# VectorE, in place of TensorE, subtracts the row maximum of the odd heads' scores, and the order of all queues is drawn up anew

## The chip, the core and the metric

The kernel runs on one core of a Trainium2 chip, as one launch. The core has five engines, each with an instruction queue of its own that it works off in order: TensorE (PE: matrix products, into the banks of PSUM), VectorE (DVE), ScalarE (ACT), GpSimd (POOL) and SyncE (SP, which here only issues transfers). The metric is the device time of one execution in microseconds (us); lower is better.

## What is computed

The input is 32 sequences of 128 tokens with 128 features. First comes one cross attention (16 heads of 8 features, 4 key heads) on a normed input, and then a stack of six layers. Each layer is a local attention with 16 heads of 64 features and a feed-forward layer. The change touches the softmax of the local attention:

```python
def local_attention(q, k, v):            # windows of 32 tokens
    ...
    bk2, bv2 = (look(bk), look(bv))      # each window sees itself and the one before
    ...
    mask = (it < jb) | (it > jb + w) | (jb == -1)
    sim = jnp.einsum('bhwie,bhwje->bhwij', bq, bk2) * QK_SCALE
    sim = jnp.where(mask, -jnp.finfo(sim.dtype).max, sim)
    attn = jax.nn.softmax(sim, -1)
    out = jnp.einsum('bhwij,bhwje->bhwie', attn, bv2)
```

The kernel takes heads in pairs; what follows calls the second of each pair an odd head. In 64 columns there are the scores of one head's window against its own 32 keys and the 32 before.

## The kernel before

**Tiling.** The stack works on groups of four sequences (eight groups per layer), and within a group on one sequence at a time, a unit: six layers of 32 units, 192 in all. `unit` projects queries and keys (`qk`, lines 442 to 444, three matmuls of 512 columns each that share one bank), squares them on ScalarE (`sq`, L790), multiplies them by the rotary tables on VectorE (`tab`, L796, 1024 columns, the last reader of a projection's bank), adds the halves on GpSimd (`add`, L802), sums the squares on VectorE (`ss`, L805), scales (`mul`, L819), and transposes on TensorE (`tq`, L448). The values come through `y`, `yt` (L837) and a transfer into the tile `ysh`. `ffn` closes a group: residual sum (L907, L967), norm, and three gated products.

**Scores and softmax.** Two banks are set aside for scores, `sc`, one for even heads (`a` = 0) and one for odd heads (`a` = 1). ScalarE first copies the mask into both (`msk`, L860), and the matmuls of `scores` (L855) add to it. `soft(a)` then does the softmax of one bank, 128 rows by eight times 64 columns:

- `mx` (L869, VectorE): the maximum of every 64 columns, with its sign turned, into `mx`.
- Even heads: `exb` (L877, ScalarE): eight exponentials of 64 columns, each with its column of `mx` as bias and with the sum beside it.
- Odd heads (`FOLD = (1,)`): `fold` (L871, TensorE): one matmul of the identity `identr` with `mx`, broadcast to 512 columns, which adds the negative maximum to the scores in their bank. `ex` (L873, ScalarE): one exponential of 512 columns from the bank to the tile `pr`. `sm` (L882, VectorE): the sums.
- Both: reciprocal (`rl`, L883, VectorE), product (`pl`, L884, GpSimd), transpose of 32x32 blocks (`pt`, L886, VectorE). Then `av` (L899, TensorE, 56 small matmuls) multiplies by the values.

The tiles `pr` and `PT` are three each, `mx` four. Projections, transposes and products share five banks, `pj`.

**Order.** No engine's order is the order of the program's text. Each operation is put down as `S.op` with the tiles that it reads and writes; `Sched.run` then plays the whole kernel with a table of costs (`COST`: engine, time for which it holds the engine, time to the result) and writes every engine's queue in the order that this gives. Whenever an engine is free it takes, among the operations that are ready and get their tiles, the one due first. An operation is due at the number of its unit plus a shift from `LATER`, by its name and number (`mx1`) or by its name (`mx`), and 0 if neither is there. `KEEP` says how many of the five shared banks an operation must leave free. Tiles of a pool are given out in the order in which the text asks for them. On the chip the queues are fixed, and semaphores do the waiting.

Of the kernel before, what the change touches and what calls it, by code (L numbers as in the profile page):

```python
# [16 lines left out]
P = 128  # L17
# [10 lines left out]

COST = dict(
    ax=("PE", 0.4, 0.64), axh=("ACT", 0.52, 0.62), axl=("DVE", 0.6, 0.7),  # L30
    qk=("PE", 0.72, 0.94), sq=("ACT", 0.53, 0.63), ss=("DVE", 0.6, 0.68), tab=("DVE", 1.14, 1.22), add=("POOL", 1.27, 1.3), ta=("DVE", .63, .72), adda=("POOL", 1.1, 6),
    mxs=("POOL", 0.25, 0.29), dmx=("DVE", 0.42, 0.5), dnw=("DVE", 0.36, 0.44), ln=("ACT", .2, .24), ep=("ACT", .2, .24), nw=("POOL", 0.31, 0.33),
    mul=("POOL", 1.01, 1.06), tq=("PE", 0.43, 0.66), evq=("ACT", 0.51, 0.61), evk=("ACT", .5, .62),
    y=("PE", 0.72, 0.94), yt=("ACT", 0.52, 0.62), dm=("SP", 0.58, 7.0), xph=("ACT", .6, .7), xpl=("ACT", .6, .7), dw=("SP", .62, 3.5), dr=("SP", .62, 4.5),
    msk=("ACT", 0.54, 0.63), sc0=("PE", .52, .75), sc1=("PE", .52, .75), mx=("DVE", 0.6, 0.68), fold=("PE", 0.3, 0.5), ex=("ACT", .51, .62), exb=("ACT", 1.17, 1.3),
    sm=("DVE", 0.6, 0.68), rl=("DVE", 0.13, 0.21), pl=("POOL", 1.02, 1.06), pt=("DVE", 0.62, 0.7), av=("PE", 1.92, 2.02), sc=("PE", 0.72, 0.9),
    res=("DVE", .63, .72), psh=("SP", 1.65, 3.5), st=("DVE", 0.79, 0.87), ag=("DVE", .35, .40), xn1=("POOL", 1.08, 1.1),
    eps=("POOL", .22, .26), lnf=("ACT", .22, .21), epf=("ACT", .22, .21), nwf=("POOL", 0.18, 0.24), xn=("ACT", 1.55, 1.65), nmr=("POOL", .18, .24), nmg=("POOL", .2, .26), ysq=("ACT", .2, .24), xn2=("POOL", 1.08, 1.1),
    ptn=("PE", .46, .70), xnh=("ACT", .51, .62), xnl=("DVE", .60, .66), gate=("PE", 0.72, 0.93), gel=("ACT", 0.63, 0.7),
    pa=("PE", 0.72, 0.93), um=("DVE", 0.68, 0.76), w2=("PE", 0.67, 0.9), res2=("DVE", .63, .72), xo=("POOL", 1.3, 1.3),  # L40
    io=("SP", .62, 3.5), iox=("SP", 1.1, 4.0), ldw=("SP", 0.5, 4.0),
    bip=("PE", 1.3, 1.5), bid=("DVE", .25, .3), tb=("DVE", 1.1, 1.1), w1a=("ACT", .78, .9), w1b=("ACT", .39, .5),
    w1c=("POOL", .95, .95), qkh=("ACT", .54, .64), qkl=("POOL", 1.3, 1.3), wvp=("PE", .46, .70), wve=("ACT", .49, .60),
    mp=("PE", 0.5, 0.7), mh=("ACT", .28, .38), ml=("DVE", .33, .42),
    xst=("DVE", 0.8, 0.87), xag=("DVE", .30, .35), xnw=("POOL", .20, .20), xtr=("PE", 0.54, 0.68), xev=("ACT", .49, .60),
    xpj=("PE", 0.98, 1.15), hil=("ACT", .58, .70), lof=("DVE", .66, .75), pv=("PE", .90, 1.1), vt=("DVE", .25, .30),
    td=("PE", .90, 1.1), abs=("ACT", .52, .65), lnb=("ACT", .55, .64), mkb=("DVE", .42, .42), tbm=("DVE", .95, 1.0),
    xsc=("PE", 0.4, 0.58), xmx=("DVE", .86, .95), xsb=("POOL", 1.04, 1.07), xex=("ACT", .55, .65), xpa=("PE", 1.1, 1.3),
    xrl=("DVE", 0.17, 0.25), xat=("DVE", .21, .29), pwm=("PE", .90, 1.1), xrs=("DVE", .63, .70),
)  # L50

LATER = dict(y=0.5, iox=1.9, xsc=-0.5, evk=-0.25, tab0=-3.2, pv=1.95, sq2=1.0, xex=1.25, ss1=3.95, rl0=5.15,
    bip=-2.05, add3=3.75, ss2=-1, xpa=0.25, tq2=-2, sq3=0.5, ax=-0.3, tab2=0.75, ysq=1.15, tq1=0.75, gate2=0.6,
    mx1=2.7, mul2=2.5, fold0=-2.5, y3=3.75, exb0=6.3, pl1=4.3, add0=1.25, tq0=2.2, nwf=1.6, msk0=0.7, y1=3.75,
    evq0=-0.7, add1=-0.35, mxs=-1.75, yt2=2.0, td=-0.95, ep=0.5, y0=3.2, gate1=-0.75, xsb=-1.05, mul1=1.3, rl1=3.75,
    qk0=-0.25, ln=-2.5, sq=-0.15, av=2.7, pwm=2.0, evq2=0.3, xpj=-1.25, xmx=3.95, ex1=1.15, y2=2.15, xnl=3, lof=0,
    tq=1.25, mp=-2.9, tab1=3.85, qk2=-1.45, yt3=-0.2, exb01=3.65, exb00=-0.35, qk1=0.4, xrl=-0.75, yt1=1.75, pl0=-1.4,
    sm0=-1.1, ml=-1, xn2=1.0, gel1=0.65, um2=-0.95, gate0=0.1, io=0.5, tab=-0.25, abs=-0.9, add=6.25, pa2=1.75,
    evq1=-0.5, xst=-0.75, xo=4, gel0=3, xag=0.9, gel2=-1.5, xev=3.65, tq3=2.85, pt=3.15, axh=-2, mx0=-0.45, lnb=3.95,
    pa1=0.1, bid=1.45, sq0=0.2, ex=2.05, nw=3.1, yt0=-0.8, ss=3.2, axl=-1.2, xn=0.1, xtr=-1.15, w1a=1.9, dm2=0.75,  # L60
    ss0=-2.15, msk1=-0.95, ldw=1, gate=-1.4, msk=-1.75, lnf=1.75, um1=4.4, vt=-0.25, w1c=-1.3, ss3=-1.5, dm3=3.95,
    tb=1.5, psh=-0.2, fold1=-2.2, tab3=0.15, xn1=0.0, pa=0.35, ptn=-0.65, mx=3.1, exb=0.75, dm1=4, evq3=-1.4,
    evq=3.05, res2=-1.5, xnh=-0.25, wvp=0.4, fold=0.45, rl=-0.95, dm=0.35, epf=-1.9, qk=0.25, pl=-2.1, sm=1.1,
    w2=1.15, sc0=0.0, mul=-0.5, tbm=0.25, mkb=2.6, xrs=-0.75, dnw=-0.5, mh=0.75, um=2, qkl=1.2, um0=-0.25, ag=-0.4,
    mul3=0.2, qkh=-1.55, xat=3, eps=-1.5, nmr=0.0, pa0=3.1, yt=2, gel=0.5, st=0.75, hil=0.05, sq1=-0.75, wve=3,
    nmg=0.75)

KEEP = dict(qk=0, y=0, gate=0, pa=0, xtr=0, xpj=1, pv=1, td=1, xsc=0, wvp=2, mp=2, bip=2, sc0=0, tq=0, ptn=0, ax=0,
    w2=1)
ONEBANK = ("pj", "sc", "po")  # L70
LAT = dict(PE=.06, ACT=.05, DVE=.08, POOL=.16, SP=.08)

# [13 lines left out]
class Sched:  # L86
# [150 lines left out]
def body(ctx: ExitStack, tc: tile.TileContext, x, ctx_in, fside, mask_in, xWq, xWk, xWv, xWo, xtw,  # L237
         Wqkv, q_scale, k_scale, Wo, ln_g, ln_b, W1, b1, W2, b2, cst, x1d, out):
    nc = tc.nc
# [11 lines left out]
    def tl(tag, shape, dt=F32):  # L251
        return mem.tile(shape, dt, tag=tag, name=tag)

    S = Sched()
    S.back = lambda: nc.scalar.preload_act_table_set("natural_log_exp_and_others")  # L255

    def pool(name, n, shape, dt=F32, inorder=True):
        S.pool(name, [lambda d, i=i: tl(f"{name}_{i}_", shape, d or dt) for i in range(n)], inorder)
# [29 lines left out]
        pool(name, 4, [P, 32])  # L288
    for name in ("xm", "sm"):
        pool(name, 6, [P, 8])  # L290
    pool("mx", 4, [P, 8], F32R)
    for name in ("nv", "ny", "nw", "av", "ay", "aw"):
        pool(name, 2, [P, 8])
    for name in ("n", "a"):
# [7 lines left out]
    ident = cs[:, 0:128]  # L302
# [474 lines left out]
    def unit(l, g, j, w, G, pri):  # L777
        xh, xl = G["x"]
        ss = Buf("ss")
        rts = []  # L780
        tab = w["tab"]
# [62 lines left out]
        sc = [Buf("sc"), Buf("sc")]  # L844
# [19 lines left out]
        def r8(b):  # L864
            return b.t.rearrange("p (a c) -> p a c", c=64)

        def soft(a):
            s, mx, pr, sm, PT = sc[a], Buf("mx"), Buf("pr"), Buf("sm"), PTs[a]
            S.op("mx", lambda: nc.vector.tensor_reduce(mx.t, r8(s), axis=AX.X, op=ALU.max, negate=True), pri, [s], [mx], k=a)  # L869
            if a in FOLD:  # L870
                S.op("fold", lambda: nc.tensor.matmul(s.t, identr, mx.t.unsqueeze(2).to_broadcast([P, 8, 64]), start=False,  # L871
                                                      stop=True, skip_group_check=True), pri, [mx, s], [s], k=a)
                S.op("ex", lambda: nc.scalar.activation(pr.t, s.t, AF.Exp), pri, [s], [pr], table="E", k=a)  # L873
            else:
                def pieces(h):
                    for i in range(4 * h, 4 * h + 4):
                        nc.scalar.activation(r8(pr)[:, i], r8(s)[:, i], AF.Exp, bias=mx.t[:, i:i + 1].bitcast(F32),  # L877
                                             accum_out=sm.t[:, i:i + 1])
# [171 lines left out]
```

## Time and profile before

Three runs: median 2971.93 us (2967.31 to 2973.36).

| | |
|---|---|
| profiled execution, its own time | 2971.38 us |
| its span, first to last instruction | 2969.6 us |
| granted TensorE clock, mean | 0.993 |
| `fold` L871, all 192: TensorE busy | 75.97 us |
| `ex` L873, all 192: ScalarE busy | 120.01 us |
| `mx` L869, all 384: VectorE busy | 252.54 us |
| `exb` L877, all 3072: ScalarE busy | 503.28 us |

The profile is of one execution, taken by the hardware. "Busy" is the time covered by an engine's instructions, overlaps counted once; PE stands for the matmuls and PEld for TensorE's weight loads, which overlap them. Matmuls are pipelined and their ends are modelled. In a group of instructions the columns are the line, engine, operation, output and inputs, shapes and number, then the busy time and the mean duration in ns, and then the idle time of the engine just before them with what ended it. The chain that ended last is followed back from the last instruction, at each step to what released it. The cross attention takes about the first 290 us; the six layers follow.

### The profile page before, as it was taken

Reading aid. Unit: us, or ns where it says so; the run is one execution under the profiler, and the core shown is the slowest. Engines: PE = TensorE matmul, PEld = TensorE weight load, DVE = VectorE, ACT = ScalarE, POOL = GpSimd, SP = SyncE. Lnnn points to the kernel's source line nnn. Section 1 sums busy time; section 2 is a strip of 40 time slices with the busy share of each in tenths; the row PEclk is TensorE's granted clock in tenths of the full one; section 3 lists DMA queues with packets and bytes.
Section 4 is the critical chain, followed back from the end, with each engine's and each line's share of the span. In section 5 each row is a group of like instructions: output and inputs, shape, how many; then the busy total and the mean of one; then the engine's idle time right before and its main releaser. Section 6 shows DMA issues by size and latency. Waiting matters only on the chain.

```text
span 2969.6 us, 116618 instructions
## 1 busy us (share of the span) xinstructions
PE 2885.9 (97%) x47695; PEld 2282.8 (77%) x47695; DVE 2522.5 (85%) x5155; ACT 2641.4 (89%) x7679; POOL 2540.0 (86%) x2950
## 2 busy tenths in 40 slices
PE   8999999999999999999999999999999999999997
PEld 5666788787777777787787777777777887877775
DVE  6778988888988888988889888888888888888883
ACT  6887899999989989999999899899899999999885
POOL 7667989888988888989898898888889888899883
PEclk9999999999999999999999999999999999999998
DMA  4101455555645455555455555455555455455453
GB/s 116 33 17 34 85 93 88 81 87 98 99 81 87 80 88 101 95 86 89 78 92 104 84 92 86 74 93 100 87 86 91 76 91 96 80 101 91 81 97 62
DMA packets 216889, 250.84 MB, mean 84 GB/s; under 512 B 90623, under 2 KB 111395, under 8 KB 216355
## 3 DMA queue, kind: packets, MB, share of 16 engines
q1 hardware_dynamic: 215442, 242.94, 48.2%
q8 instruction: 376, 6.16, 1.1%
q14 instruction: 159, 1.29, 0.2%
q10 hardware_dynamic: 912, 0.44, 0.1%
HBM read 25.31 MB, written 4.19 MB: 10 GB/s over the span
## 4 chain that ended last, share of the span: by engine, by line
PE 83%; ACT 6%; DMA 5%; issue 3%; POOL 2%; DVE 2%; SPq 0%; POOLq 0%; DVEq 0%; ACTq 0%
PE bank__68 L899 11%; PE bank__67 L855 4%; PE bank__66 L855 4%; PE bank__61 L448 3%; PE bank__65 L448 3%; PE bank__62 L448 3%; PE bank__63 L448 3%; PE bank__64 L448 3%; PE bank__64 L442 3%; PE bank__65 L442 3%; PE bank__61 L442 3%; PE bank__63 L442 3%; PE bank__62 L442 3%; PE bank__65 L444 2%; PE bank__65 L443 2%
## 5 line engine op out<-in xcount | busy, mean ns | idle before, releaser
L860 ACT COPY bank__66<-mask 128x512 f32<-128x512 f32 x192 | 122.1, 636 | 5.4 <-PE bank__66 L374 4.7
L860 ACT COPY bank__67<-mask 128x512 f32<-128x512 f32 x192 | 122.1, 636 | 1.5 <-PE bank__67 L374 0.9
L255 ACT ACT_TABLE_LOAD x48 | 61.6, 1283 | 0.8
L944 ACT ACT_TABLE_LOAD x48 | 61.6, 1283 | 0.8
L727 ACT ACTIVATE ysh__96<-ysh__96 128x512 f32<-128x512 f32 x64 | 40.9, 639 | 11.7 <-POOL ysh__96 L725 11.4
L907 DVE TENSOR_TENSOR xt<-bank__68,xt 128x512 f32<-128x512 f32 x48 | 32.6, 680 | 11.7 <-PE bank__68 L899 11.7
L727 ACT ACTIVATE wch__97<-wch__97 128x512 f32<-128x512 f32 x16 | 10.1, 633 | 8.8 <-POOL wch__97 L725 8.8
L967 DVE TENSOR_TENSOR xt<-bank__64,xt 128x512 f32<-128x512 f32 x12 | 8.3, 691 | 6.8 <-PE bank__64 L963 6.8
L974 POOL TENSOR_TENSOR raw__50456<-raw__50456,xt 128x512 f32<-128x512 f32 x1 | 1.3, 1261 | 13.9 <-DVE xt L967 13.9
L727 ACT ACTIVATE wch__98<-wch__98 128x512 f32<-128x512 f32 x16 | 10.2, 639 | 3.0 <-POOL wch__98 L725 2.9
L967 DVE TENSOR_TENSOR xt<-bank__65,xt 128x512 f32<-128x512 f32 x11 | 7.5, 686 | 5.5 <-PE bank__65 L963 5.4
L884 POOL TENSOR_TENSOR pr__51149<-pr__51149,sm__51156 128x512 f32<-128x512 f32 x1 | 1.0, 1043 | 10.9 <-DVE sm__51156 L883 10.9
L727 ACT ACTIVATE wch__100<-wch__100 128x512 f32<-128x512 f32 x16 | 10.3, 643 | 0.1
L409 ACT ACTIVATE ny__51394<-nv__51392 128x4 f32<-128x4 f32 x1 | 0.2, 205 | 11.4 <-POOL nv__51392 L404 11.4
L727 ACT ACTIVATE wch__99<-wch__99 128x512 f32<-128x512 f32 x16 | 10.2, 641 | 0.0
L448 PE MATMUL bank__64<-cs,ysh__96 128*128 128x128 f32 x60 | 9.3, 278 | 0.3 <-ACT ysh__96 L727 0.2
L967 DVE TENSOR_TENSOR xt<-bank__62,xt 128x512 f32<-128x512 f32 x10 | 6.9, 692 | 3.0 <-PE bank__62 L963 3.0
L730 ACT COPY ysh__96<-bank__61 128x512 f32<-128x512 f32 x12 | 7.1, 594 | 2.4 <-PE bank__61 L448 2.3
L730 ACT COPY ysh__96<-bank__64 128x512 f32<-128x512 f32 x15 | 8.9, 595 | 0.3 <-ACT ysh__96 L730 0.3
L730 ACT COPY ysh__96<-bank__63 128x512 f32<-128x512 f32 x13 | 7.7, 595 | 1.6 <-PE bank__63 L448 1.5
L448 PE MATMUL bank__65<-cs,ysh__96 128*128 128x128 f32 x52 | 8.5, 290 | 0.6 <-ACT sq__2222 L692 0.3
L448 PE MATMUL bank__61<-cs,sq__51404 128*128 128x128 f32 x4 | 1.6, 474 | 7.7 <-ACT sq__51404 L927 7.7
(24629 smaller groups left out, 15800.3 us busy)
## 6 DMA issues: line engine op xcount, KB each, us to landing
xt<-xt SPq DMA_DIRECT2D x96, 112.0 KB, 2.5
xt<-in_x SPq DMA_DIRECT2D x16, 128.0 KB, 4.0
x_scratch<-xt SPq DMA_DIRECT2D x8, 256.0 KB, 2.3
xt<-xt SPq DMA_DIRECT2D x96, 15.0 KB, 2.3
stg__699<-in_L_ffn_Wo SPq DMA_DIRECT2D x1, 512.0 KB
stg__11210<-in_L_ffn_Wo SPq DMA_DIRECT2D x1, 512.0 KB
stg__19197<-in_L_ffn_Wo SPq DMA_DIRECT2D x1, 512.0 KB
stg__27184<-in_L_ffn_Wo SPq DMA_DIRECT2D x1, 512.0 KB
```

The source lines that it names most:

```text
L255: S.back = lambda: nc.scalar.preload_act_table_set("natural_log_exp_and_others")
L442: nc.tensor.matmul(pt, lh, rh, start=True, stop=False)
L443: nc.tensor.matmul(pt, lh, rl, start=False, stop=False)
L444: nc.tensor.matmul(pt, ll, rh, start=False, stop=True)
L448: nc.tensor.transpose(dst[:, k * P:(k + 1) * P], srcs[k], ident if eye is None else eye)
L727: S.op("xex", lambda: nc.scalar.activation(sm.t, sm.t, AF.Exp), pri, [sm], [sm], table="E")
L730: S.op("xev", lambda: nc.scalar.copy(sm.t, pt.t), pri, [pt, sm], [sm])
L855: nc.tensor.matmul(s4[a][32 * c:32 * c + 32, half, wd, lo:64], q[r, c * P + 32 * wd:c * P + 32 * wd + 32], k[r, c * P + 32 * wd - 32 + lo: ...
L860: S.op("msk", lambda b=b: nc.scalar.copy(b.t, mask), pri, (), [b], k=a)
L899: nc.tensor.matmul(po.t[32 * wd:32 * wd + 32, j * P:(j + 1) * P], p5[a][:, half, wd, blk, :], ysh[0].t[:, u * 512 + h * P:u * 512 + (h + 1 ...
L907: S.op("res", lambda: nc.vector.tensor_tensor(xv(g), hv(po.t), xv(g), op=ALU.add), pri, [po, X[g]], [X[g]])
L944: S.op("gel", lambda: nc.scalar.activation(u.t[0:n], pg.t[0:n], AF.Gelu, bias=b1c.t[0:n, 1, i:i + 1]), pri, [pg, b1c], [u], table="G", k=i)
```

## The change

The odd heads' `fold` on TensorE goes. In its place `sub`, on VectorE, reads the scores from the bank, adds the negative maximum and writes the tile `pr`; `ex` then works in place in `pr`. The tile `identr` goes, and `mx` is an ordinary float32 tile. The tables `COST`, `LATER` and `KEEP` are replaced, so that every queue's order is another; what the other operations do is unchanged.

```diff
 COST = dict(
     ...
-    qk=("PE", 0.72, 0.94), sq=("ACT", 0.53, 0.63), ...
+    qk=("PE", 0.735, 0.94), sq=("ACT", 0.53, 0.63), ...
-    mxs=("POOL", 0.25, 0.29), dmx=("DVE", 0.42, 0.5), dnw=("DVE", 0.36, 0.44), ... nw=("POOL", 0.31, 0.33),
-    mul=("POOL", 1.01, 1.06), tq=("PE", 0.43, 0.66), ...
+    mxs=("POOL", 0.32, 0.33), dmx=("DVE", 0.42, 0.5), dnw=("DVE", 0.4, 0.48), ... nw=("POOL", 0.25, 0.27),
+    mul=("POOL", 1.01, 1.06), tq=("PE", 0.44, 0.66), ...
-    y=("PE", 0.72, 0.94), ...
+    y=("PE", 0.735, 0.94), ...
-    ... mx=("DVE", 0.6, 0.68), fold=("PE", 0.3, 0.5), ex=("ACT", .51, .62), exb=("ACT", 1.17, 1.3),
-    ... av=("PE", 1.92, 2.02), sc=("PE", 0.72, 0.9),
+    ... mx=("DVE", 0.6, 0.68), sub=("DVE", .61, .69), ex=("ACT", .51, .62), exb=("ACT", 1.17, 1.3),
+    ... av=("PE", 1.97, 2.05), sc=("PE", 0.77, 0.87),
     ...

-LATER = dict(y=0.5, ... mx1=2.7, ... ex1=1.15, ... fold1=-2.2, ...
+LATER = dict(y=2.1, ... mx1=3.1, ... ex1=0.7, ... tab0=-4.8, ... tab1=3.7, ... tab2=-0.75, ... tab3=0.75, ...
+    # some 170 entries, nearly all with other values; there is none for `sub`

-KEEP = dict(qk=0, y=0, gate=0, pa=0, xtr=0, xpj=1, pv=1, td=1, xsc=0, wvp=2, mp=2, bip=2, sc0=0, tq=0, ptn=0, ax=0,
-    w2=1)
+KEEP = dict(qk=0, y=0, gate=0, pa=0, xtr=0, xpj=1, pv=1, td=1, xsc=0, wvp=2, mp=2, bip=2, sc0=0, tq=0, ptn=0, ax=1,
+    w2=0)
...
-    pool("mx", 4, [P, 8], F32R)
+    pool("mx", 4, [P, 8])
...
-    identr = tl("identr", [P, P], F32R)
-    nc.vector.tensor_copy(identr, ident)
...
             if a in FOLD:
-                S.op("fold", lambda: nc.tensor.matmul(s.t, identr, mx.t.unsqueeze(2).to_broadcast([P, 8, 64]), start=False,
-                                                      stop=True, skip_group_check=True), pri, [mx, s], [s], k=a)
-                S.op("ex", lambda: nc.scalar.activation(pr.t, s.t, AF.Exp), pri, [s], [pr], table="E", k=a)
+                S.op("sub", lambda: nc.vector.tensor_tensor(r8(pr), r8(s), mx.t.unsqueeze(2).to_broadcast([P, 8, 64]),
+                                                            op=ALU.add), pri, [mx, s], [pr], k=a)
+                S.op("ex", lambda: nc.scalar.activation(pr.t, pr.t, AF.Exp), pri, [pr], [pr], table="E", k=a)
```

More of the change, by code (lines that the diff above doesn't have):

```diff
@@ L30 @@
     ax=("PE", 0.4, 0.64), axh=("ACT", 0.52, 0.62), axl=("DVE", 0.6, 0.7),
[L31 to L36, printed above, removed]
+    qk=("PE", 0.735, 0.94), sq=("ACT", 0.53, 0.63), ss=("DVE", 0.6, 0.68), tab=("DVE", 1.14, 1.22), add=("POOL", 1.27, 1.3), ta=("DVE", .63, .72), adda=("POOL", 1.1, 6),
+    mxs=("POOL", 0.32, 0.33), dmx=("DVE", 0.42, 0.5), dnw=("DVE", 0.4, 0.48), ln=("ACT", .2, .24), ep=("ACT", .2, .24), nw=("POOL", 0.25, 0.27),
+    mul=("POOL", 1.01, 1.06), tq=("PE", 0.44, 0.66), evq=("ACT", 0.51, 0.61), evk=("ACT", .5, .62),
+    y=("PE", 0.735, 0.94), yt=("ACT", 0.52, 0.62), dm=("SP", 0.58, 7.0), xph=("ACT", .6, .7), xpl=("ACT", .6, .7), dw=("SP", .62, 3.5), dr=("SP", .62, 4.5),
+    msk=("ACT", 0.54, 0.63), sc0=("PE", .52, .75), sc1=("PE", .52, .75), mx=("DVE", 0.6, 0.68), sub=("DVE", .61, .69), ex=("ACT", .51, .62), exb=("ACT", 1.17, 1.3),
+    sm=("DVE", 0.6, 0.68), rl=("DVE", 0.13, 0.21), pl=("POOL", 1.02, 1.06), pt=("DVE", 0.62, 0.7), av=("PE", 1.97, 2.05), sc=("PE", 0.77, 0.87),
     res=("DVE", .63, .72), psh=("SP", 1.65, 3.5), st=("DVE", 0.79, 0.87), ag=("DVE", .35, .40), xn1=("POOL", 1.08, 1.1),
@@ L50 @@
 )
[L52 to L66, printed above, removed]
@@ L68 @@
-KEEP = dict(qk=0, y=0, gate=0, pa=0, xtr=0, xpj=1, pv=1, td=1, xsc=0, wvp=2, mp=2, bip=2, sc0=0, tq=0, ptn=0, ax=0,
-    w2=1)
+LATER = dict(y=2.1, iox=-0.95, xsc=-0.95, evk=-0.25, tab0=-4.8, pv=1.5, sq2=1.25, xex=-0.1, ss1=4, rl0=4.65, bip=-2.2,
+    add3=2.8, ss2=-1.05, xpa=0.15, sq3=0.6, ax=-1.3, tab2=-0.75, ysq=-0.65, mx1=3.1, mul2=2.35, fold0=-2.5, y3=3.85,
+    exb0=6.3, pl1=2.9, add0=0.75, tq0=2.35, nwf=1.6, y1=3.55, add1=-0.75, mxs=-1.95, ep=0, y0=3.2, qk0=-0.05, av=2.25,
+    pwm=2.5, xpj=-1.6, xmx=3.8, ex1=0.7, y2=1.0, xnl=0.5, tab1=3.7, qk2=-2.45, yt3=-0.7, exb01=3.95, qk1=0.4,
+    xrl=-2.1, yt1=1.05, pl0=-1.3, sm0=-1.1, ml=2.85, gate0=2.0, io=-0.35, abs=-1.6, add=5.35, pa2=3.25, gel2=-1.05,
+    xev=-0.75, tq3=3.0, axh=-0.75, pa1=0.9, nw=2, yt0=-2.2, xtr=-1.3, ss0=-2.15, lnf=1.5, ss3=-2.4, psh=-1.75,
+    xnh=0.25, wvp=-0.25, dm=-2.15, qk=0.5, dnw=-0.7, mul3=-0.3, pa0=2.05, gel=4, sq1=-1.45, nmg=-1, evq1=-1.8, sc=4,
+    xat=3.0, rl1=0.85, sc0=0.5, mp=0.8, sm1=3.85, pt1=3.0, fold1=0.25, axl=2.1, tab=0.75, ldw=-0.75, pt0=2.05,
+    sq0=0.5, exb00=-1.35, mx0=0.65, ex=-2, qkh=0.15, pl=-2, tq1=-1.65, mul0=-1.5, vt=0, dm0=-1.5, lof=1.5, gel1=-0.35,
+    ag=0.25, epf=0.4, gate2=-2, evq2=2.0, gel0=0.9, eps=2.8, tq2=-0.4, dm2=0.75, sc1=-1.2, um=3.65, um2=-0.75,
+    evq0=0.5, exb=-2.25, sq=-0.2, fold=3, evq3=-2.4, lnb=1.5, nmr=-1.35, xo=0.05, pt=-0.25, yt2=0.15, tb=-0.25,
+    sm=-0.25, pa=0.5, bid=1.25, msk0=-1.75, xsb=0.65, res2=2.9, mul1=0.6, um0=-0.75, wve=-0.75, mkb=2.1, tq=1.5,
+    tab3=0.75, xn1=0.75, w1a=-1.0, w2=0.7, rl=2.8, mx=3, mh=-1.6, qkl=0.25, msk1=-1.55, tbm=-2.5, xn2=-0.25, hil=-0.2,
+    xn=0.5, xrs=4, mul=0.2, ln=0, res=1, st=-0.45, xag=0.65, yt=0.5, msk=1.4, evq=-1.0, ptn=0, um1=-0.5, dm1=-0.55)
@@ L876, in pieces @@
                     for i in range(4 * h, 4 * h + 4):
-                        nc.scalar.activation(r8(pr)[:, i], r8(s)[:, i], AF.Exp, bias=mx.t[:, i:i + 1].bitcast(F32),
+                        nc.scalar.activation(r8(pr)[:, i], r8(s)[:, i], AF.Exp, bias=mx.t[:, i:i + 1],
                                              accum_out=sm.t[:, i:i + 1])
```

## The prediction

> **What bounds the kernel now.** I read the shares of the engines first, and then the chain that ended last.
>
> ```profile
> span 2969.6 us, 116618 instructions
> PE 2885.9 (97%) x47695; PEld 2282.8 (77%) x47695; DVE 2522.5 (85%) x5155; ACT 2641.4 (89%) x7679; POOL 2540.0 (86%) x2950
> PE 83%; ACT 6%; DMA 5%; issue 3%; POOL 2%; DVE 2%; SPq 0%; POOLq 0%; DVEq 0%; ACTq 0%
> ```
>
> TensorE is busy for 97% of the span and holds 83% of the chain; VectorE holds 2%. A share over the whole span mixes stages, so the busy time by stretch comes next (columns: stretch, its length, busy time and instructions of PE, PEld, DVE, ACT, POOL, then the granted clock, DMA share and GB/s).
>
> ```profile
> 0.00:290.00 290.00, 269.07 (x1931) 184.73 (x1934) 217.50 (x1323) 225.19 (x465) 207.97 (x280) 0.97 0.19 49
> 740.00:1190.00 450.00, 443.81 (x7750) 356.53 (x7749) 392.64 (x660) 411.25 (x1228) 396.54 (x454) 1.00 0.55 90
> 1190.00:1640.00 450.00, 445.17 (x7862) 357.59 (x7861) 396.15 (x658) 414.86 (x1236) 401.01 (x463) 1.00 0.55 90
> 2530.00:2970.00 440.00, 410.33 (x7055) 327.48 (x7054) 346.41 (x578) 370.47 (x1103) 348.94 (x402) 0.98 0.49 85
> ```
>
> In an inner stretch (1190 to 1640) TensorE is idle for 4.8 of 450 us, while VectorE is idle for 54 (12%), ScalarE for 35 and GpSimd for 49. So TensorE sets the pace, but the other three are close behind: the work moves from an engine at 99% to one at 88%. Only the first stretch and the last leave TensorE idle for about 7%. The clock is granted in full, so there is nothing to win there.
>
> The order of time says what a busy TensorE means, and what one fold costs in it (start, duration, instruction):
>
> ```profile
> 1405.45 0.40 PE L444 MATMUL bank__63<-wch__18599,xl__23638 128*128 128x512 f32 x1
> 1405.69 0.39 PE L442 MATMUL bank__62<-wch__18822,xh__23637 128*128 128x512 f32 x1
> ...
> 1382.25 0.39 PE L444 MATMUL bank__62<-wch__18599,xl__22654 128*128 128x512 f32 x1
> 1382.48 0.38 PE L871 MATMUL bank__66<-mx__23545,identr 128*128 128x512 f32 x1
> 1382.69 0.40 PE L442 MATMUL bank__63<-wch__18822,xh__22653 128*128 128x512 f32 x1
> ```
>
> A matmul is recorded for 0.38 to 0.40 us, but the next one starts 0.21 to 0.24 us later. Without a fold between them the step from L444 to L442 is 0.24 us; with it, 0.44, and the fold's own step is 0.21 us, about half of what it is recorded with. Busy time overstates what its removal is worth.
>
> **The change, part by part.** *Removed: 192 folds*, six layers of 32 sequences. At 0.21 us of the stream that is 192 x 0.21 = 40 us. The upper end is their whole busy time, 75.97 us by the busy time of L871 over the span, or 0.40 us each; it would be right if the moments at which TensorE stands before a fold or behind it went as well. I take 40, because nearly all folds stand between back-to-back matmuls as the one above, and keep 76 for the range.
>
> [...]
>
> *Added: 192 subtractions on VectorE.* Each reads 128x512 from a bank and a broadcast column from SBUF and writes SBUF. The nearest rows are other two-operand instructions with a bank as source:
>
> ```profile
> 1415.05 0.69 DVE L869 TENSOR_REDUCE mx__24228<-bank__67 128x8 fp32r<-128x512 f32 x1 [0.35 <-PE bank__66 L855]
> 1415.65 0.68 DVE L933 TENSOR_TENSOR nl__24176<-bank__64,nh__24175 128x512 fp32r<-128x512 f32 x1
> 1416.25 0.68 DVE L805 TENSOR_REDUCE ss__23908<-sq__24226 128x8 f32<-128x512 f32 x1
> L907 DVE TENSOR_TENSOR xt<-bank__68,xt 128x512 f32<-128x512 f32 x48 | 32.6, 680 | 11.7 <-PE bank__68 L899 11.7
> ```
>
> It is recorded with 0.68 us, and the next start comes 0.60 us later. I take 0.61 for the step, since L907 reads its second operand in pieces as the subtraction does: 192 x 0.61 = 117 us on VectorE (131 at 0.68). Per inner stretch of 450 us that is 32 x 0.61 = 20 us, so that VectorE's idle time falls from 54 to 34 us, and its share rises from 88% to 92%.
>
> What of it reaches TensorE? If VectorE's idle time takes all of it, nothing. If none of it is covered, all 117 us. For the first speaks ScalarE, which has 35 idle us in the same stretch without TensorE idling for more than 4.8: an engine at 92% is no bound here. For the second speaks that VectorE works in order. What queues behind a subtraction is L796 (1.2 us each, four in a unit, the last reader of a projection's bank), the transposes L886 that the attention's matmuls L899 wait for, and the sums L805 that GpSimd waits for. Both rows stand near the first end, but three engines would now be at 90% or more where ScalarE was alone. I take a fifth, 0.2 x 117 = 23 us, and keep both ends.
>
> *The exponential* L873 now reads SBUF. It is 120.01 us for 192 instructions, 0.625 us each; the nearest row is L727, an exponential of the same size in place in SBUF:
>
> ```profile
> L727 ACT ACTIVATE ysh__96<-ysh__96 128x512 f32<-128x512 f32 x64 | 40.9, 639 | 11.7 <-POOL ysh__96 L725 11.4
> ```
>
> That is 0.014 us more, 192 x 0.014 = 3 us of ScalarE in six layers, half a microsecond per inner stretch beside 35 idle ones. I count zero; uncovered it is 3 us. [...]
>
> *Waits.* The fold's wait for the maximum goes from TensorE, and none comes instead: the maximum is on VectorE's own queue just ahead. The bank of the odd heads is free after the subtraction and no longer after the exponential, which is 0.6 us or more sooner for the mask's copy L860 of the next unit. The tile `pr` is taken by the subtraction and not by the exponential, so it is held longer by one such step, out of three tiles. Both are under a microsecond of slack in units 14 us apart; I count them at nothing. If the earlier bank is worth something it lies in the 76; if the tile stops VectorE, that is in the 117. At the end of the kernel, where nothing covers, the path has 0.68 for 0.38 us once, 0.3 us. The tile `identr`, one copy at the start, goes too, beside the loads.
>
> *The order.* All due times, some costs and two reserves (`ax` 1 for 0, `w2` 0 for 1) are new, so every queue moves, SP's and GpSimd's among them; the number of DMAs and their sizes stay. Its worth is not to be read from a row. Bounds: the five inner stretches have 33 us of TensorE's idle time (2240 us less 2206.5 busy), and a perfect order would win these. If they idled like the last stretch (29.7 of 440, 6.7%), 117 us would be lost. I take nothing: the inner stretches are within 2% of full, and most of what can happen is a loss that comes through VectorE, which I have in the fifth.
>
> *Sum.* The profiled execution took 2971.38 us, 1.8 beyond its span and 0.5 under the median of 2971.93, so they can stand for each other. 2971.4 - 40 + 23 = **2954 us**, 0.6% faster.
>
> **Rivals.** *VectorE's queue holds TensorE (slower).* The subtraction's due time has no entry among the new `LATER` values, so it is due at the unit's own time, while its maximum is due 3.1 later: it goes as soon as it can, ahead of whatever L796 stands ready. Banks of projections are then read later, TensorE runs out of banks and idles. The price is s x 117 - 40, where s is the share that reaches TensorE; it decides from s = 0.34. At s = 0.75 it is +48: 3019 us, TensorE's busy share at (2885.9 - 76) / 3017 = 93%, which is what the last stretch shows (410.33 of 440). For it: three engines near 90%, and 12% idle time on VectorE that is not where it is needed. Against it: VectorE's 2% of the chain.
>
> *All covered (faster still).* VectorE's idle time takes everything (s = 0), and the waits around the folds go too: 2971.4 - 40 = 2931 down to 2971.4 - 76 = 2895. For it: ScalarE at 92% without harm. Against it: a share of VectorE that would then be (2522.5 + 131) / 2900 = 91% over the whole span.
>
> *A draw.* s at 0.3 to 0.4: the 40 us are given back exactly, 2966 to 2977.
>
> **How the numbers follow.** About 0.2% (6 us) can be told from no change here. Forecast, s from 0 to 0.3, 2931 to 2966: 0.38. All covered and more, 2895 to 2931: 0.12. Draw: 0.10. VectorE's queue or a worse order, above 2977: 0.40. So faster 0.50, same 0.10, slower 0.40. The range reaches from 2905, ten above the best bound, to 3020, the slower rival's price; about 2 in 10 are left, most of them above. The forecast's own range is 2931 to 2966.
>
> **What would show it.** Right: no line of folds, TensorE's busy time near 2810, its share near 95%, VectorE near 2650 with a subtraction at 0.68 us, inner stretches some 3 us shorter for the same work, and VectorE's idle time ahead of L796 shrunk. Wrong on the slow side: TensorE's idle time in the inner stretches above 5%, with VectorE or ScalarE named as the releaser, and L796 or L886 on the chain. Wrong on the fast side: TensorE above 96% busy after all. If the subtraction's step is 0.8 us or more, or L873 grew by over 0.05 us, my rows were the wrong ones. If the first 290 us change by more than 5 us, the order is at work and not the subtraction, which does not occur there.

## The result, and the profile after

The changed kernel takes 2992.38 us (median of four runs, 2984.23 to 2997.12), the kernel before 2971.47 us beside it: a ratio of 1.0071, with a 95% interval of 1.0055 to 1.0086. It is 21 us slower, where 2954 us had been forecast. The profiled execution took 2991.85 us. In what follows a run's distance in us is its ratio less one, times 2971.5.

The page of the changed kernel, span and shares of the engines:

```profile
span 2990.1 us, 116648 instructions
PE 2874.7 (96%) x47503; PEld 2250.7 (75%) x47503; DVE 2673.9 (89%) x5346; ACT 2641.6 (88%) x7679; POOL 2539.8 (85%) x2950
```

The folds are gone (192 matmuls fewer) and VectorE has 151 us more. TensorE's recorded busy time fell by 11 us only, though its folds had 76 us of it. Overlaps count once, and a fold that is recorded with 0.38 us takes 0.21 us of the stream, so no more than some 41 us could go; what filled the rest was not traced. The chain of this page covers only about 6% of the span, and nothing is read from it; further down the chain is read from a kernel in which only the instruction was changed.

The changed kernel's busy time by stretch (columns as in the prediction):

```profile
0.00:290.00 290.00, 273.43 (x1837) 188.38 (x1837) 215.21 (x1313) 222.14 (x449) 200.34 (x272) 0.94 0.18 47
1190.00:1640.00 450.00, 437.79 (x7711) 347.83 (x7710) 414.62 (x683) 409.25 (x1225) 393.27 (x449) 1.00 0.54 90
290.00:2530.00 2240.00, 2171.18 (x38121) 1723.34 (x38121) 2064.98 (x3383) 2023.66 (x6052) 1968.06 (x2248) 1.00 0.53 88
```

In the inner stretch VectorE is at 92%, as forecast, and TensorE idles for 12.2 us, where it had been 4.8. Over the whole middle, 290 to 2530, TensorE's idle time is 68.8 us after 33.5 before. Not one of the other three engines is above 93% in these rows, and yet TensorE waits more than twice as much.

VectorE in order of time, changed kernel (start, duration, instruction):

```profile
1454.94 0.68 DVE L866 TENSOR_REDUCE mx__24530<-bank__67 128x8 f32<-128x512 f32 x1
1455.54 1.21 DVE L793 TENSOR_TENSOR t__24539<-bank__65,tabs__10901 128x1024 f32<-128x1024 f32 x1
1456.67 0.68 DVE L868 TENSOR_TENSOR pr__24553<-bank__67,mx__24530 128x512 f32<-128x512 f32 x1
1457.27 0.67 DVE L802 TENSOR_REDUCE ss__24429<-sq__24544 128x8 f32<-128x512 f32 x1
```

The subtraction (L868) is recorded with 0.68 us and gives way 0.60 us later, both as forecast. No instruction waits between these four. A table product (L793) stands between the maximum and its subtraction.

The exponential L870 of the changed kernel, ScalarE's busy time over the span:

```profile
0.00:2991.00 2991.00, 126.62 (x192) 0.99 0.50 84
```

It is 0.659 us each, after 0.625: 6.6 us in all.

A mean over a stretch hides where in a group the idle time lies, so here is one group of four units in three parts: two that make up most of it, and the end, in which the last products of the feed-forward layer are summed. The kernel before:

```profile
1427.80:1460.00 32.20, 32.20 (x623) 25.94 (x622) 29.74 (x52) 29.19 (x93) 30.45 (x34) 1.00 0.65 103
1460.00:1476.80 16.80, 15.74 (x289) 12.11 (x288) 14.52 (x22) 15.06 (x42) 15.57 (x20) 1.00 0.47 77
1476.80:1482.40 5.60, 5.60 (x42) 5.13 (x41) 3.26 (x7) 5.57 (x17) 1.83 (x4) 1.00 0.00 0
```

The same group after the change:

```profile
1444.80:1480.00 35.20, 35.13 (x664) 27.93 (x665) 34.03 (x60) 31.00 (x96) 31.39 (x35) 1.00 0.59 100
1480.00:1497.40 17.40, 15.96 (x271) 11.92 (x261) 16.78 (x24) 16.20 (x46) 16.50 (x22) 1.00 0.57 102
1497.40:1502.60 5.20, 5.20 (x41) 4.70 (x40) 2.90 (x7) 5.19 (x16) 3.77 (x6) 1.00 0.31 69
```

Before, VectorE was idle for 7.1 us in this group, of which 2.3 lay in the last 5.6 us, in which this group has no maximum left to take. In the 49 us that have the softmax, VectorE was at 90%, ScalarE at 90% and GpSimd at 94%: 4.7 idle us of VectorE, in pieces, for the 2.4 us that four subtractions need. After the change VectorE is at 97% in that part (50.8 of 52.6 us) and still at 56% at the end. These are single groups, and this one, with 57.6 us from closing sum to closing sum, is longer than the changed kernel's mean of 55.2.

### The profile page after: what moved, and what is told of

Read it like the earlier page. It is cut to its first block, busy times and chain, and to the rows that moved or that the text cites. A ratio compares the mean times of both kernels' runs of the same rounds, so it can differ in the third digit from the quotient of the medians.

```text
span 2990.1 us, 116648 instructions
## 1 busy us (share of the span) xinstructions
PE 2874.7 (96%) x47503; PEld 2250.7 (75%) x47503; DVE 2673.9 (89%) x5346; ACT 2641.6 (88%) x7679; POOL 2539.8 (85%) x2950
## 5 line engine op out<-in xcount | busy, mean ns | idle before, releaser
L724 ACT ACTIVATE ysh__94<-ysh__94 128x512 f32<-128x512 f32 x64 | 40.8, 639 | 6.8 <-POOL ysh__94 L722 6.7
L727 ACT COPY ysh__94<-bank__62 128x512 f32<-128x512 f32 x21 | 12.4, 590 | 3.7 <-PE bank__62 L445 3.6
L964 DVE TENSOR_TENSOR xt<-bank__62,xt 128x512 f32<-128x512 f32 x16 | 10.9, 684 | 4.0 <-PE bank__62 L960 3.5
L445 PE MATMUL bank__62<-cs,ysh__94 128*128 128x128 f32 x84 | 14.0, 293 | 0.3 <-ACT rt__851 L669 0.2
L445 PEld LDWEIGHTS bank__62<-cs,ysh__94 128*128 128x128 f32 x84 | 10.2, 149 | 3.3 <-ACT ysh__94 L727 0.8
L727 ACT COPY ysh__94<-bank__64 128x512 f32<-128x512 f32 x16 | 9.5, 595 | 0.9 <-PE bank__64 L445 0.8
L445 PE MATMUL bank__64<-cs,ysh__94 128*128 128x128 f32 x64 | 10.0, 278 | 0.1
L445 PEld LDWEIGHTS bank__64<-cs,ysh__94 128*128 128x128 f32 x64 | 7.2, 141 | 3.3 <-issue 1.6
L445 PE MATMUL bank__65<-cs,sq__51402 128*128 128x128 f32 x4 | 1.6, 476 | 7.6 <-ACT sq__51402 L924 7.6
L727 ACT COPY ysh__94<-bank__65 128x512 f32<-128x512 f32 x9 | 5.3, 594 | 3.7 <-PE bank__65 L445 3.7
```

Source lines behind the costliest of these rows:

```text
L445: nc.tensor.transpose(dst[:, k * P:(k + 1) * P], srcs[k], ident if eye is None else eye)
L724: S.op("xex", lambda: nc.scalar.activation(sm.t, sm.t, AF.Exp), pri, [sm], [sm], table="E")
L727: S.op("xev", lambda: nc.scalar.copy(sm.t, pt.t), pri, [pt, sm], [sm])
L964: S.op("res2", lambda: nc.vector.tensor_tensor(xv(g), hv(py.t), xv(g), op=ALU.add), pri, [py, X[g]], [X[g]])
```

## The experiments

In the edits `S.op(...)` keeps its place when its instruction is left out (`lambda: None`), so the order of all other instructions is the one that it was. "Old tables" are `COST`, `LATER` and `KEEP` of the kernel before, "new tables" those of the changed kernel.

### The edit and the order, each alone

The subtraction with the old tables, from the changed kernel:

```diff
-COST, LATER, KEEP = # the new tables; sub=("DVE", .61, .69)
+COST, LATER, KEEP = # the old tables, with sub=("DVE", .61, .69)
```

> The changed kernel's subtraction with the tables (COST, LATER, KEEP) of the kernel before; only the entry of fold in COST gives way to that of sub. Theory Q (VectorE's queue: 192 subtractions take 117 us of VectorE, about half of that reaches TensorE, and the tables matter little): about 2992 us, as the changed kernel. Theory T (the new tables are the loss, the subtraction by itself wins): 2945 to 2960 us.

Measured: 3050.39 us, ratio 1.0264 [1.0251, 1.0277], 78 us slower, far above both expectations.

The fold with the new tables, from the kernel before:

```diff
-COST, LATER, KEEP = # the old tables; fold=("PE", 0.3, 0.5)
+COST, LATER, KEEP = # the new tables, with fold=("PE", 0.3, 0.5)
```

> The kernel before with its fold, under the changed kernel's tables; the entry of sub in COST gives way to that of fold. Theory Q: within 6 us of 2971 us, since no subtraction is there. Theory T: 3005 to 3035 us, the loss of the tables without the gain of the 40 us of TensorE's stream. Its first 290 us answer for the cross attention alone: Theory T expects the 9 us by which the changed kernel is late at the end of the first group here too.

Measured: 3002.66 us, 1.0100 [1.0086, 1.0115], 30 us slower, about as theory T had it. Each form is bad with the other's tables, because a new cost makes the planner draw a new order throughout. Neither run says what the instruction is worth. For that the order has to stand still.

### The unchanged order: the fold taken out, then the subtraction put in

```diff
-S.op("fold", lambda: nc.tensor.matmul(s.t, identr, ...), pri, [mx, s], [s], k=a)
+S.op("fold", lambda: None, pri, [mx, s], [s], k=a)
```

> The kernel before with the fold's matmul left out and every queue otherwise in the same order; the odd heads' exponential takes scores without their maximum subtracted. It prices the removal alone. If a fold is worth its own step of 0.21 us: 2931 us. If it is worth its whole record and the waits around it: 2895 us. If the other engines hold the pace at once: above 2955 us. Theories Q and T both expect about 2931.

Measured: 2960.14 us, 0.9966 [0.9954, 0.9978], a gain of 10 us where the stream's steps made 40. Its busy time in the middle:

```profile
290.00:2530.00 2240.00, 2189.72 (x38701) 1753.89 (x38698) 1964.89 (x3267) 2048.12 (x6135) 1989.52 (x2277) 1.00 0.54 89
```

TensorE is busy for 17 us less than before in the same 2240 us (2206.5) and the idle time grew by as much, to 50.3. The other three engines are within 7 us of where they were.

The same work is compared between the closing sums of the first group and the last (L967 before; 47 of the 48 groups lie between them). The kernel before, and without the fold:

```profile
379.10:2963.90 2584.80, 2531.98 (x44255) 2032.19 (x44253) 2223.65 (x3698) 2337.46 (x6966) 2244.39 (x2572) 1.00 0.53 89
382.90:2956.80 2573.90, 2501.97 (x44069) 2004.39 (x44067) 2220.44 (x3699) 2332.16 (x6966) 2242.94 (x2572) 0.99 0.54 89
```

The groups take 10.9 us less. TensorE is busy for 30 us less, and idle for 71.9 us where it had been 52.8. So of the 41 us that the steps of the folds make, 10.9 came out at the end and 19 went into waiting; the rest is still recorded as busy time. The chain of this kernel's page, where TensorE had 83% before:

```profile
PE 72%; ACT 8%; POOL 7%; issue 4%; DMA 4%; DVE 4%; SPq 0%; POOLq 0%; DVEq 0%; ACTq 0%
```

The granted clock is no more than a small part of it. The twelve runs without the fold lie between 2954.38 us at a mean clock of 0.993 and 2976.95 us at 0.987, so a lower clock and a longer time go together. At 0.993 alone the gain is some 14 us (three runs with a mean of 2956.2 us, six of the kernel before with 2970.5), which leaves 27 of the 41 us missing.

On top of this, the subtraction in the same place of VectorE's queue, right behind the odd heads' maximum and in place in the bank (so the exponential still reads the bank):

```diff
+def top():
+    nc.vector.tensor_reduce(mx.t, r8(s), ..., negate=True)
+    if a in FOLD:
+        nc.vector.tensor_tensor(r8(s), r8(s), mx.t.unsqueeze(2).to_broadcast([P, 8, 64]), op=ALU.add)
+S.op("mx", top, pri, [s], [mx], k=a)
```

> The kernel before, every queue in the same order, the fold's matmul left out, and the subtraction done by VectorE right behind the odd heads' maximum, in place in the scores' bank, so that the exponential still reads the bank. It prices the move without any new order. Theory Q: 2985 to 3000 us. Theory T: 2940 to 2960 us. Against the kernel without fold it gives what 117 us of VectorE cost where nothing else changes.

Measured: 2991.43 us, 1.0072 [1.0060, 1.0084], 21 us slower: the result of the whole change, in the old order. Against the run without the fold the subtractions cost 31 us of their 117, a share of 0.27. The chain of this kernel's page, and then a piece of it in order of time (start, duration, engine, tile, line):

```profile
PE 60%; DVE 23%; ACT 5%; issue 4%; POOL 4%; DMA 3%; SPq 0%; POOLq 0%; DVEq 0%; ACTq 0%
```

```profile
1268.71 0.67 DVE mx__21274 L870
1269.38 0.60 DVE nl__21222 L936
1269.98 0.59 DVE ss__20954 L803
1270.57 0.62 DVE PT__21300 L889
1271.19 0.59 DVE mx__21309 L870
1271.78 0.02 issue
1271.80 0.04 DVE bank__67 L868
1271.84 0.57 issue
1272.41 1.22 DVE t__21314 L794
1273.62 1.13 DVE t__21345 L794
1274.76 1.18 DVE ss__21149 L803 x2
```

VectorE's part of the chain goes from 2% before to 23%. In this piece it holds the chain for nearly 10 us, almost back to back, and pieces like it come in most groups: a queue with next to nothing free in it, of table products (L794), sums (L803) and transposes (L889), as the slower rival had named them. The subtraction (L868, whose step the chain puts down mostly to "issue") is one more of them.

The share once more, with the fold left in place and one more reduction of 512 columns behind each odd maximum (192 x 0.60 = 114 us of VectorE):

```diff
+    if a in FOLD:
+        nc.vector.tensor_reduce(spare, mask.rearrange("p (a c) -> p a c", c=64), axis=AX.X, op=ALU.max)
```

> The kernel before in its order, fold in place, with one more reduction of 512 columns on VectorE (of the mask's tile in SBUF, into a tile that nobody reads) right behind each odd maximum: 192 steps of 0.59 us, 114 us of VectorE, that nothing depends on. It prices VectorE's time with TensorE as it was. If TensorE covers VectorE's idle time (the fifth of the prediction): 2975 to 2995 us. If VectorE's place in the order and not TensorE's share sets the price, as much as the subtraction cost without the fold: plus 31, 3003 us. The fold itself follows the maximum as before and does not wait for the extra reduction.

Measured: 2994.99 us, 1.0069 [1.0052, 1.0086], 20.5 us slower, a share of 0.18 of the 114 us, as the first of the two expectations had it. (VectorE's recorded busy time grew by 92 us.)

### Why 40 us of TensorE's stream brought 10

First the other direction, a second matmul (with a matrix of zeros) behind each fold:

```diff
+for w in (identr, zeror):
+    nc.tensor.matmul(s.t, w, mx.t.unsqueeze(2).to_broadcast([P, 8, 64]), ...)
```

> The kernel before, every queue in the same order, with a second matmul behind each fold, the same columns against a matrix of zeros. It adds to TensorE what the removal took away, 192 steps of 0.21 us, 41 us. Theory P (TensorE sets the pace alone, and the missing 30 us of the removal were lost otherwise): plus 35 to 45 us, about 3010. Theory V (four engines hold the pace together, and one of them gives or takes about a quarter of its own change): plus 8 to 15 us, about 2981.

Measured: 2993.81 us, 1.0074 [1.0059, 1.0090]: 22 us for the 41 us that are added. That lies between the two theories. So with the folds in place TensorE does bound the kernel, at about half price. The pair of matmuls in order of time, and then the 47 groups:

```profile
1228.33 0.38 PE L875 MATMUL bank__67<-mx__20657,identr 128*128 128x512 f32 x1
1228.55 0.38 PE L875 MATMUL bank__67<-mx__20657,zeror 128*128 128x512 f32 x1
378.50:2986.90 2608.40, 2569.62 (x44441) 2066.66 (x44439) 2228.46 (x3698) 2348.32 (x6966) 2242.47 (x2572) 1.00 0.53 88
```

TensorE is busy for 38 us more than before and idle for 14 us less (38.8): part of the second matmul went where TensorE had stood idle.

Then each of the other engines is lightened alone, the folds in place: ScalarE by the odd heads' mask copy, GpSimd by the odd heads' product, VectorE by most of each odd sum.

```diff
-S.op("msk", lambda b=b: nc.scalar.copy(b.t, mask), ...)
+S.op("msk", lambda b=b, a=a: nc.scalar.copy(b.t, mask) if a == 0 else None, ...)
```

> The kernel before, same order, without the copy of the mask into the odd heads' bank (192 copies of a step of 0.52 us on ScalarE, 100 us less; the odd heads' scores then add to what the bank held). Theory P: no change, 2965 to 2972 us, since ScalarE is not the bound. Theory V: a quarter of 100, about 2945 us.

```diff
-S.op("pl", lambda: nc.gpsimd.tensor_tensor(...), ...)
+S.op("pl", lambda: None if a in FOLD else nc.gpsimd.tensor_tensor(...), ...)
```

> The kernel before, same order, without the odd heads' product on GpSimd (192 products of a step of 1.0 us, 192 us less; the odd heads' probabilities stay unscaled). Theory P: no change, 2965 to 2972 us. Theory V: a sixth to a quarter of 192, since so large a piece runs out of waits to remove, 2922 to 2940 us.

```diff
-nc.vector.tensor_reduce(sm.t, r8(pr), axis=AX.X, op=ALU.add)
+nc.vector.tensor_reduce(sm.t, r8(pr)[:, :, 32:34], axis=AX.X, op=ALU.add)
```

> The kernel before, same order, fold in place, with the odd heads' sums on VectorE taken over 2 of every 64 columns (192 reductions of 16 in place of 512 elements, some 0.5 us less each, 96 us of VectorE). Theory P: no change, 2965 to 2972 us. Theory V: about as much as a subtraction costs with the other sign, a quarter of 96, 2940 to 2950 us.

Measured: ScalarE 2974.90 us, 1.0005 [0.9995, 1.0015]; GpSimd 2971.67 us, 0.9994 [0.9984, 1.0003]; VectorE 2969.95 us, 0.9986 [0.9976, 0.9996]. By the recorded busy times 89, 192 and 85 us went from these engines, and that brings 0, 2 and 4 us, as theory P had it; the quarter of theory V did not come. None of the three alone bounds the kernel before.

The same three edits with the fold left out, first one at a time:

> The kernel before in its order, fold's matmul left out (no maximum subtracted in the odd heads) and the odd heads' sums on VectorE over 2 of every 64 columns, 96 us of VectorE less. The removal of the folds alone gave 10 of the 41 us. Theory D (VectorE is the next limit and kept the other 30): 2930 to 2940 us. Theory L (what kept them is the length of the dependent chains, in which all engines have a part; no single engine): 2950 to 2958 us.

> The same without fold, with VectorE's sums whole, and without the mask's copy into the odd heads' bank (ScalarE 100 us less; the odd heads' scores add to what the bank held). Theory A (ScalarE is the next limit): 2930 to 2940 us. Theory L or D: 2950 to 2962 us.

> The same without fold, and without the odd heads' product on GpSimd (192 us of GpSimd less; odd heads unscaled). Theory G (GpSimd is the next limit): 2930 to 2940 us. Theory L, D or A: 2950 to 2962 us.

Measured: with short sums 2954.24 us, 0.9941 [0.9925, 0.9956]; without the odd mask 2962.52 us, 0.9958 [0.9945, 0.9972]; without the odd product 2960.25 us, 0.9953 [0.9937, 0.9968]. In us that is 17.5, 12.5 and 14 of gain, after 10 for the missing fold alone. No single engine took TensorE's place. Added to the 10, the three further gains make 24 us.

All three at once, with the fold left out:

> The kernel before in its order without the folds, and at the same time with VectorE 96 us lighter (odd heads' sums over 2 of 64 columns), ScalarE 100 us lighter (no mask's copy into the odd heads' bank) and GpSimd 192 us lighter (no product for odd heads). The odd heads' exponential has a scale of 0.0001, so that its values stay small; odd heads' results have no meaning. Theory M (three engines stand full side by side, and relieving one leaves the other two): 2925 to 2940 us, the whole 41. Theory L (the length of dependent chains and transfers keeps the rest): 2945 to 2955 us.

Measured: 2934.42 us, 0.9870 [0.9848, 0.9893], a gain of 38.6 us, near the 40 of the prediction and more than the 24 that the steps add up to one by one. Its middle, then its 47 groups, and its chain:

```profile
290.00:2530.00 2240.00, 2199.19 (x38900) 1763.65 (x38899) 1893.63 (x3289) 1986.41 (x6011) 1837.22 (x2127) 1.00 0.54 90
378.00:2927.90 2549.90, 2492.87 (x44070) 2001.14 (x44067) 2126.15 (x3698) 2246.35 (x6781) 2057.11 (x2386) 1.00 0.54 90
PE 85%; ACT 4%; DVE 4%; issue 3%; DMA 2%; POOL 2%; SPq 0%; POOLq 0%; DVEq 0%; ACTq 0%
```

TensorE's idle time in the middle is back from 50.3 to 40.8 us (33.5 before the change), in the groups from 71.9 to 57.0, and TensorE has the chain again. This points to the other three engines together as what kept back most of the folds' worth. Two runs are missing for a full proof: the three lightened together with the folds in place, and the three in pairs. One at a time, with the folds in place, they brought 6 us in sum, so most of the 38.6 should be the folds', but that was not measured. Nor did any run draw an order for a kernel without folds; the 10 us are what the removal is worth in an order that was drawn up around the folds.

### The order again

The changed kernel with short sums, to see whether VectorE alone now bounds it:

```diff
-nc.vector.tensor_reduce(sm.t, r8(pr), axis=AX.X, op=ALU.add)
+nc.vector.tensor_reduce(sm.t, r8(pr)[:, :, 32:34], axis=AX.X, op=ALU.add)
```

> The changed kernel in its own order with the odd heads' sums over 2 of every 64 columns, 96 us of VectorE less. In the kernel before the same cut was worth 3 us. Theory Q (the subtraction has made VectorE the limit): 25 to 50 us less than the changed kernel, 2942 to 2967. Theory T (the new order is what costs, and VectorE still has room): within 8 us of the changed kernel, 2984 to 2992.

Measured: 2991.32 us, 1.0059 [1.0039, 1.0080], no gain that can be told from the changed kernel's 1.0071. That is what theory T expected: in the new order, VectorE's load alone is not what costs. So the subtraction was taken out of the changed kernel, in its own order (the exponential then reads the bank):

```diff
-S.op("sub", lambda: nc.vector.tensor_tensor(r8(pr), r8(s), ...), pri, [mx, s], [pr], k=a)
+S.op("sub", lambda: None, pri, [mx, s], [pr], k=a)
-S.op("ex", lambda: nc.scalar.activation(pr.t, pr.t, AF.Exp), pri, [pr], [pr], table="E", k=a)
+S.op("ex", lambda: nc.scalar.activation(pr.t, s.t, AF.Exp), pri, [pr], [pr], table="E", k=a)
```

> The changed kernel in its own order without the subtraction: the odd heads' exponential takes the scores from the bank, without their maximum subtracted. Theory Q (the subtraction's time on VectorE, where it stands between the maximum and the exponential, is the loss): 2950 to 2970 us. Theory T (the new order is worse for all engines, whatever the subtraction does): 2980 to 2992 us.

Measured: 2984.99 us, 1.0052 [1.0035, 1.0069]. Read as it stands, the subtraction costs some 6 us in its own order (the two intervals overlap), where it cost 31 in the old one, and the kernel with neither fold nor subtraction is 15 us slower than before, where the old order without the fold was 10 faster. But this run does not do the work of that one. In the plan the odd heads' bank is free once the subtraction is over, so ScalarE copies the next unit's mask into it at once, and here the exponential still has to read it:

```profile
1409.46 0.63 ACT L857 COPY bank__66<-mask 128x512 f32<-128x512 f32 x1
1410.13 0.60 ACT L869 ACTIVATE pr__23710<-bank__66 128x512 f32<-128x512 f32 x1
```

In 190 of the 192 units the mask's copy comes first in this way, the exponential reads the wrong values, and TensorE's next scores wait for it: 18.4 us in all, where in the changed kernel they wait 7.7 us for the exponential. So neither the 6 us of the subtraction nor the 26 (15 and 10) that would be left for the order is a measured price; how the new order's loss divides is not shown.

Where the changed kernel loses its time can be read from the closing sums of the groups, `res2` (columns: line and tiles, number, shortest, median and longest in ns, first and last start; read the two starts). The kernel before, the changed kernel, and the fold with the new tables (its last sum stands in the row of another bank, at 2996.5):

```profile
L967 DVE TENSOR_TENSOR xt<-bank__65,xt x11: 641/691/692, 379.1 to 2963.9; 128x512 f32<-128x512 f32 x11
```

```profile
L964 DVE TENSOR_TENSOR xt<-bank__63,xt x10: 673/691/692, 387.8 to 2984.4; 128x512 f32<-128x512 f32 x10
```

```profile
L966 DVE TENSOR_TENSOR xt<-bank__63,xt x12: 640/691/692, 399.2 to 2961.6; 128x512 f32<-128x512 f32 x12
```

The subtraction in the old order:

```profile
L970 DVE TENSOR_TENSOR xt<-bank__65,xt x11: 640/692/693, 378.5 to 2980.7; 128x512 f32<-128x512 f32 x11
```

After the cross attention and four units of 192 the changed kernel is 8.7 us late, and the fold with the new tables 20.1; the subtraction in the old order is not. The 47 groups that follow take 2584.8 us before, 2596.6 in the changed kernel and 2602.2 with the subtraction in the old order. So of the changed kernel's 20.5 us (profiled executions) 8.7 are lost at the start and 11.8 in the groups, and in the groups the new order is 5.6 us better for the subtraction than the old one (one execution of each). Not all of the 8.7 need be the order's: the granted clock of the first 290 us is 0.94 there and 0.97 before, and the old order without folds and with short sums, at 0.92 in these 290 us, had its first sum at 391.2:

```profile
L966 DVE TENSOR_TENSOR xt<-bank__65,xt x11: 639/692/692, 391.2 to 2954.7; 128x512 f32<-128x512 f32 x11
```

The changed kernel with the three lightenings together:

> The changed kernel in its own order, subtraction in place, with VectorE 96 us lighter (short sums), ScalarE 100 us lighter (no mask's copy into the odd bank) and GpSimd 192 us lighter (no odd product); the odd heads' exponential has a scale of 0.0001, and odd heads' results have no meaning. Theory M (engines full side by side): 2935 to 2960 us, as far down as the kernel before without folds went. Theory T (order of TensorE's own queue): 2975 to 2990 us.

Measured: 2974.52 us, 1.0014 [1.0002, 1.0026], just below theory T's range, 17 us faster than the changed kernel and 43 behind the old order with the same three and no fold. How these 43 divide between the subtraction and the order is open, and what else the new order waits for was not found.

Last, both forms with due times and reserves searched anew (`LATER`, `KEEP`): the fold with the new tables' costs and 0.25 for the fold itself, and the subtraction starting from the new tables.

```diff
-COST = dict(qk=("PE", 0.72, 0.94), ... fold=("PE", 0.3, 0.5), ... av=("PE", 1.92, 2.02), sc=("PE", 0.72, 0.9), ...
+COST = dict(qk=("PE", 0.735, 0.94), ... fold=("PE", 0.25, 0.5), ... av=("PE", 1.97, 2.05), sc=("PE", 0.77, 0.87), ...
-LATER = dict(y=0.5, ... fold1=-2.2, ... tab0=-3.2, ...
+LATER = dict(abs=5.4, ... fold1=0.2, ... tab0=-3.85, ...   # all entries
-KEEP = dict(qk=0, y=0, ... wvp=2, mp=2, bip=2, sc0=0, tq=0, ptn=0, ax=0, w2=1)
+KEEP = dict(abs=2, axh=1, ... evq=2, ... sq=2, tab=1, ... w2=1, wvp=2, ... yt=1)
```

> The kernel before with its fold and the changed kernel's COST (fold at 0.25 us), and due times and reserves searched anew for it. Theory Q: faster than the kernel before, 2945 to 2965 us, and 15 to 30 us faster than the searched order of the subtraction. Theory O (only the order was poor): not faster than the searched order of the subtraction.

> The changed kernel with due times and reserves searched anew for it, with the same costs and effort as for the fold. Theory Q: 2970 to 2985 us, a few us better than the changed kernel and not better than the kernel before. Theory O: 2945 to 2960 us.

Measured: the fold 2952.64 us, 0.9930 [0.9908, 0.9951], 21 us faster than before and the best kernel here that does all the work; the subtraction 3012.63 us, 1.0135 [1.0111, 1.0159], worse than the changed kernel, against both expectations. The middle of the fold's new order:

```profile
290.00:2530.00 2240.00, 2211.92 (x38812) 1777.56 (x38801) 1966.85 (x3272) 2039.01 (x6136) 1991.73 (x2278) 1.00 0.55 89
```

The same instructions as before, and TensorE idles for 28.1 us in place of 33.5. An order alone was worth between -21 and +30 us for the fold, and the four orders tried for the subtraction lie between 2991 and 3050 us. That none for the subtraction goes lower is not shown.

## Why the prediction was wrong, step by step

**The removal was the step that failed.** 192 x 0.21 = 40 us assumed that TensorE sets the pace alone, "an engine at 92% is no bound here". At an unchanged order the folds' removal brought 10 us. The steps of the stream were read rightly: in the run with two matmuls for each fold the second starts 0.21 or 0.22 us after the first in 28 of 32 pairs between 1190 and 1640 us. What was wrong is the assumption that the time so freed comes out at the end. Three more engines run nearly full beside TensorE (88%, 92% and 89% of the inner stretch before), and without the folds it waits for one or the other of them: its share of the chain falls from 83% to 72% while theirs together grows from 10% to 19%, and its idle time in the 47 groups grows by 19 us. Lightening TensorE, or TensorE and one other, moved the end by 10 to 17.5 us; lightening all four, by 38.6. That the three hold it together is shown by this last run as far as it goes; which pair would do, and what an order drawn for a kernel without folds would bring, is open. VectorE's 12% of idle time, which argued for cover, is a mean over a whole stretch. Leaving out the end of a group changes it little (VectorE at 90% in place of 87% in the group shown), so the mean's size was not the fault, but the use of it as cover.

**The subtraction's step was right, its share a little low.** 0.60 us and 117 us in all, as forecast. The share that reaches TensorE was put at 0.2 and measured 0.27 (31 us for 23), or 0.18 with the fold in place. The sum with the measured terms is -10 + 31 = +21 us. That is the time of the old order with the subtraction, and by chance also that of the changed kernel.

**The slower rival had the right mechanism, as far as the old order shows it.** VectorE's queue of L796, L886 and L805 (other numbers in other kernels) is what appears on the chain of the subtraction in the old order; the changed kernel's own chain cannot be read. The rival had been said to decide from a share of 0.34, which is 40/117; with the removal at its true worth it decides from 10/117 = 0.09. The price of 3019 us for it was too high: TensorE's idle time in the inner stretch is 12.2 of 450 us, 2.7% and not the 5% named as the sign.

**The order was counted at nothing, and the totals agree with that by chance.** The old order with the subtraction gives 1.0072, the new one 1.0071. But the old one loses 17.4 us in the 47 groups and nothing ahead of them, the new one 11.8 and 8.7. Of the sign that had been named for the order, a change of the first 290 us by more than 5 us, there is something: TensorE is busy for 4.4 us more there, and the first group ends 8.7 us late, part of which may be the lower clock. An order drawn up anew can move the time by far more than the edit, as the other tables show.

**Smaller terms.** L873 grew by 0.034 us each, below the 0.05 named as a sign against the rows, 6.6 us in all for the 3 of my row. TensorE's busy time near 2810 us was wrong by 65 (2874.7): taking off the folds' whole 76 us was not sound where their records overlap those of their neighbours (0.38 us recorded, the next start 0.21 us later), as the prediction's own remark on busy time should have told.

## What to carry to other kernels

When one engine is at 99% and three more at 88% to 92%, do not call the others' idle time cover: here lightening any one of the three brought 0 to 4 us and lightening the first 10, but all four together 39. Price a removal by leaving the instruction out with every queue's order frozen, and an addition by putting it into the frozen order: here -10 and +31, which were the price of the edit in the old order. They need not be its price in another: draw up the order anew in a run of its own, since here the order alone moved the time by as much as the edit or more. When an instruction is left out of a planned order, look whether the plan still keeps its neighbours' buffers; in one run here it did not, and its number could not be used.

## What was not expected of the hardware

A second matmul of 512 columns into the same bank starts mostly 0.21 or 0.22 us behind the first, yet 192 of them cost 22 us, 0.11 us each: the step of an instruction in the stream of the busiest engine was not its price. An exponential with its source in SBUF took 0.659 us in the changed kernel and with its source in a bank 0.625 us before, where L727 and L873 of the kernel before had differed by 0.014. The granted clock of the first 290 us went from 0.97 to 0.92 between two kernels in the same order; within the twelve runs without the fold, 0.006 less of mean clock went with 2976.95 us in place of 2954.38.
